# A delta-rule decoder layer on one core: the decay table is scaled on GpSimd, one product per head with the factors repeated along rows, instead of four ScalarE scalings

## The chip, the core and the metric

The kernel runs on one core of one Trainium2 chip. A core has five engines that each work through their own instructions in the order given to them: TensorE (PE in the profile, its weight loads PEld), VectorE (DVE), ScalarE (ACT), GpSimd (POOL) and SyncE (SP), which here only issues transfers. They meet through semaphores. The metric is the device time of one execution in microseconds (us), the median of several runs.

## The reference, cut to what matters

Four sequences of 512 tokens with 512 channels go through a gated delta-rule layer, a cross attention and a layer with self attention and eight experts. Only the first part matters here. For each of 16 heads it runs a recurrence over the tokens:

```python
def step(Sstate, inputs):
    q_t, k_t, v_t, g_t, beta_t = inputs
    retrieved = jnp.einsum('bhkv,bhk->bhv', Sstate, k_t)
    error = v_t - g_t[..., None] * retrieved
    update = k_t[..., :, None] * (beta_t[..., None] * error)[..., None, :]
    Snew = g_t[..., None, None] * Sstate + update
    o_t = jnp.einsum('bhkv,bhk->bhv', Snew, q_t)
    return (Snew, o_t)
```

`q`, `k` and `v` come from projections, a causal convolution over four tokens and SiLU; `q` and `k` are then normed to length one per head. `g` is a decay between 0 and 1, `beta` a gate.

## The kernel before, in words

**Chunks.** The recurrence is computed in chunks of 128 tokens, four to a sequence (`TB` = 4). Within a chunk the errors solve a triangular system. Its matrix is the Gram matrix of the keys, times a table of products of decays, times a factor of the row (`beta` over the squared length of the key). The matrix is inverted, and the state is carried from chunk to chunk by small matmuls.

**Pairs.** Heads are taken two at a time (`HG` = 2), so a sequence has 8 pairs and the batch 32, numbered m = 0 to 31. A pair goes through stages that are spread over several turns of the main loop:

- `stage1(m)` makes keys and queries: `conv` (L533 matmul, L541 first tap on ScalarE, L544 three taps on VectorE, L547 SiLU), the transposed keys and their squared lengths (L576 to L581), the small factor tables `rk`, `ee`, `ke`, `nr` on GpSimd (L588 to L592), the decay tables `em` (L597, a scan on VectorE, one per head), their scaling by `ee` (L602, which calls `scale`), the key products (L606), and the triangular matrix `at` (L609 on VectorE), which is stored (L610) and read back in blocks as `iA` (L673).
- `stage2_inverse(m)` inverts the 32 x 32 diagonal blocks in 31 steps of two small products each (L684, L685), then a turned copy (L691) and transfers (L690 to L698). For even m it runs on VectorE, for odd m on GpSimd (`eng` at L680).
- `stage2_values(m)` makes values and the output gate, with `conv` again (L729, L731, and L537 for the gate).
- `stage3(m)` joins the blocks of the inverse (L765 to L799) and carries the state through the four chunks: L817 (keys times state, into `ps`), L819 (`r` on VectorE), L826 (inverse times `r`), L828 (`u`, copied by ScalarE), L836 (new state's update), L839 (ScalarE, first chunk) or L841 (VectorE, `state` later), and the output matmuls L844 and L846.
- `output(m)` projects a pair (L890) and adds it to the sequence's sum (L893 or L895).

In turn m of the main loop, `stage3(m)` sets the pace, and `turns` advances beside it `output(m - 1)`, two steps of `stage1(m + 2)`, one of `stage2_values(m + 1)`, two of `inversions(m)`, and sometimes the next sequence's `prologue`. `inversions(m)` makes one and two steps of the inverse of pair m + 1 by turns, so three for each turn. So while an even-numbered pair is in `stage1`, GpSimd is inverting an odd-numbered one, and VectorE inverts while an odd-numbered pair is in `stage1`.

**Order.** On VectorE, ScalarE and GpSimd the instructions stand in the order in which the program writes them (`manual_schedule`, L977). The order on TensorE and on the SP queue is made by a scheduler when the kernel is built. `em` has two buffers, one per head; `pb`, the PSUM pool of most matmuls, has four.

`scale` makes four activations, one for each chunk of 128 columns, since ScalarE takes one factor per partition: column p * 4 + c of `ee` for chunk c of head p. `along` views a table of n columns as n blocks, each column repeated:

```python
def along(ap, n):
    return ap.unsqueeze(2).to_broadcast([P, ap.shape[1], n])
```

The same `scale` also makes `kdec` from the transposed keys (`decayed`, L626).

Of the kernel before, what the change touches and what calls it, by code (L numbers as in the profile page):

```python
# [33 lines left out]
ALU = mybir.AluOpType  # L34
# [4 lines left out]
P = 128  # L39
B, S, D = 4, 512, 512  # L40
NT = B * S // P
TB = S // P
# [56 lines left out]
def decoder(ctx: ExitStack, tc: tile.TileContext, a: dict, out: bass.AP):  # L99
    nc = tc.nc  # L100
# [13 lines left out]
    def along(ap, n):  # L114

        return ap.unsqueeze(2).to_broadcast([P, ap.shape[1], n])
# [214 lines left out]
    with ExitStack() as st:  # L331
# [55 lines left out]
        def squares(d):  # L387

            return d[:, : P * P].rearrange("c (r t) -> r c t", r=P)
# [9 lines left out]
        def scale(dst, src, by, p):  # L399

            for c in range(TB):
                nc.scalar.activation(dst[:, c, :], src[:, c, :], AF.Identity, scale=by[:, p * TB + c : p * TB + c + 1])
# [149 lines left out]
        def stage1(m):  # L552
# [31 lines left out]
            rk, ee, ke = (small.tile([P, HG * TB], F32, name=n, bufs=2) for n in ("rk", "ee", "ke"))  # L584
# [8 lines left out]
            em = []  # L593
# [5 lines left out]
                yield  # L599
            ats = []  # L600
            for p in range(HG):
                scale(em[p], em[p], ee, p)  # L602
                pk = p_b.tile([P, TB, P], F32, name="pb")
                for c in range(TB):
                    k_ = kT[p][:, c * P : (c + 1) * P]
                    nc.tensor.matmul(pk[:, c, :], k_, k_, start=True, stop=True)  # L606
                at = live.tile([P, TB, P], F32, name="at", bufs=4)
                ats.append(at)
                nc.vector.scalar_tensor_tensor(at, pk, -1.0, em[p], ALU.mult, ALU.mult)  # L609
                nc.sync.dma_start(squares(at_d[m % SLOTS][p * TB : (p + 1) * TB]), at)  # L610
                yield
# [373 lines left out]

        run(itertools.islice(start, TB + 1))
        pair0 = stage1(0)
        run(turns((start, 1), (itertools.islice(pair0, 2 * HG * 2), 1)))

        run(itertools.islice(pair0, 3 * HG + 1))  # L990
        run(turns((stage2_inverse(0), 2), (chain(pair0, turns((stage1(1), 2), (stage2_values(0), 1))), 1), (prepare(), 1)))
        begun[1] = stage2_inverse(1)
        for m in range(NP):
# [17 lines left out]
            if m + 2 < NP:  # L1011
                if (m + 2) % NHG == 0:
                    assert (m + 2) // NHG in seqs
                rest.append((stage1(m + 2), 2))
# [593 lines left out]
```

## Time and profile before

| what | value |
|---|---|
| median of 3 runs | 3767.66 us (3766.09 to 3770.12) |
| the profiled execution | 3772.63 us, of it 3770.3 us span |
| mean granted TensorE clock | 0.961 |
| ScalarE, L402 on `em` | 256 instructions, 384 to 402 ns, 50.5 to 1939.0 us |
| ScalarE, L402 on `kdec` | 256 instructions, 384 to 408 ns |
| VectorE, L597 scan of `em` | 64 of 1197 to 1444 ns |
| VectorE, L609 `at` | 64 of 668 to 693 ns |
| GpSimd, L588 `rk` | 32 of 1636 to 2492 ns |

The span runs from the first instruction to the last; the profiled execution's own time is 2.3 us more. Times in a timeline are in us from the start of the span. The delta-rule stage fills the first 2000 us or so; the rest is cross attention, self attention and experts. The duration of one instruction holds its start-up and its end, so that neighbours on one engine overlap in the records: eight L402 of 386 ns in a row take 2.45 us together, 306 ns from start to start.

### The profile page before, as it was taken

The page shows a single profiled execution, that of the slowest core. Times are in us where ns is not written, and L with a number is a line of the kernel's source. Part 1 is how long each engine was busy: PE and PEld are TensorE (multiplying, and loading weights), DVE is VectorE, ACT ScalarE, POOL GpSimd, SP SyncE. Part 2 cuts the span into 40 slices and gives each one's busy share as a digit, 9 for nine tenths or more (in the row PEclk, how much of TensorE's full clock was granted, in tenths as well). Part 3 has the DMA queues.
Part 4 walks back from the last instruction along what each step waited for, and adds up shares of the span by engine and source line. Part 5 has one row for each costly group of instructions (what it writes and reads, how often), then busy time and mean ns, then how long its engine had stood idle before and what let it go on. Part 6 is the DMA issues. An engine that isn't in the chain of part 4 may idle for free. (4 is left out here: it accounts for less than half of the span.)

```text
span 3770.3 us, 48773 instructions
## 1 busy us (share of the span) xinstructions
PE 3444.4 (91%) x16466; PEld 1927.3 (51%) x16466; DVE 2205.5 (58%) x4923; ACT 1583.7 (42%) x4379; POOL 1380.1 (37%) x1941
## 2 busy tenths in 40 slices
PE   5889999999899999999997799998999999898897
PEld 3545555555555555555554455555555555554443
DVE  5667667776677666765674466555655655554111
ACT  3444444444444444444442244444444444343121
POOL 1444554356444553455543222112112111211442
PEclk8999999999999999999998799999999999999998
DMA  5333332534244342333341445445444544446444
GB/s 157 108 100 117 103 113 85 147 101 122 85 118 126 100 122 91 116 119 118 96 127 37 157 155 162 136 148 145 141 137 137 160 147 136 147 151 209 87 84 92
DMA packets 391879, 465.54 MB, mean 123 GB/s; under 512 B 128451, under 2 KB 242115, under 8 KB 391440
## 3 DMA queue, kind: packets, MB, share of 16 engines
q1 hardware_dynamic: 380080, 438.03, 38.0%
q0 software_dynamic: 10112, 21.58, 3.1%
q8 instruction: 131, 2.15, 0.2%
q10 hardware_dynamic: 1440, 2.84, 0.2%
q14 instruction: 116, 0.95, 0.1%
HBM read 401.76 MB, written 64.81 MB: 124 GB/s over the span
## 5 line engine op out<-in xcount | busy, mean ns | idle before, releaser
L533 PE MATMUL pb<-xnT,w 128*128 128x512 f32 x2048 | 973.5, 610 | 20.3 <-issue 9.9
L533 PEld LDWEIGHTS pb<-xnT,w 128*128 128x128 f32 x2048 | 374.6, 195 | 420.2 <-issue 401.1
L544 DVE SCALAR_TENSOR_TENSOR cv<-pb,pp,cv 128x510 f32<-128x510 f32 (+2 forms) x576 | 423.3, 744 | 29.2 <-ACT cv L541 16.9
L1145 PE MATMUL pb<-c_q,hT 128*128 128x512 f32 x768 | 361.3, 609 | 6.7 <-DMA c_q<-in_c_wk_dram 3.1
L685 POOL TENSOR_TENSOR iT<-iT,iW 32x31 f32<-32x31 f32 (+15 forms) x496 | 275.8, 556 | 38.9
L684 POOL TENSOR_TENSOR iW<-iA,iT 32x31 f32<-32x31 f32 (+15 forms) x496 | 250.0, 504 | 58.8 <-DMA iA<-at_d 15.6
L890 PE MATMUL pb<-wot,og 128*128 128x512 f32 x512 | 251.0, 613 | 2.0 <-issue 1.5
L1251 PE MATMUL pw<-c_o,oT 128*128 128x512 f32 x512 | 240.9, 601 | 1.0 <-DVE oT L1243 1.0
L1145 PEld LDWEIGHTS pb<-c_q,hT 128*128 128x128 f32 x768 | 143.5, 195 | 162.3 <-issue 151.5
L1217 ACT ACTIVATE e<-pb,nm,rq 128x128 f32<-128x128 f32 (+3 forms) x256 | 157.0, 619 | 141.3 <-DVE nm L1215 112.9
L541 ACT ACTIVATE cv<-pb,pp 128x512 f32<-128x512 f32 x192 | 148.6, 774 | 158.4 <-PE pb L533 155.5
L685 DVE TENSOR_TENSOR iT<-iT,iW 32x31 f32<-32x31 f32 (+15 forms) x496 | 203.7, 411 | 17.0
L640 POOL TENSOR_TENSOR qg<-qh,row 128x512 f32<-128x512 f32 x64 | 82.7, 1292 | 357.7 <-ACT qh L547 313.3
L684 DVE TENSOR_TENSOR iW<-iA,iT 32x31 f32<-32x31 f32 (+15 forms) x496 | 185.5, 374 | 42.7 <-DMA iA<-at_d 32.1
L279 POOL TENSOR_SCALAR x_e<-x_e 128x1024 f32<-128x1024 f32 x64 | 67.2, 1050 | 340.6 <-ACT x_e L274 259.6
L588 POOL TENSOR_TENSOR rk<-ss,mhalf 128x8 f32<-128x8 f32 x32 | 66.7, 2085 | 340.5 <-DVE ss L587 339.6
L895 DVE TENSOR_TENSOR xa<-pb,xa 128x512 f32<-128x512 f32 x112 | 76.9, 687 | 195.4 <-PE pb L890 195.4
L1241 PE MATMUL po<-eT,val 128*128 128x512 f32 x320 | 169.6, 623 | 11.0 <-ACT eT L1239 8.4
L274 ACT ACTIVATE x_e<-pb,nm 128x256 f32<-128x256 f32 x256 | 118.3, 476 | 128.2 <-DVE nm L271 122.2
L1211 PE MATMUL pb<-kT,qT 128*128 128x256 f32 (+3 forms) x576 | 162.6, 409 | 0.0
L1513 PE MATMUL pb<-w_gu,eT 128*128 x312 | 142.9, 602 | 3.5 <-issue 3.5
L547 ACT ACTIVATE qh<-cv 128x512 f32<-128x512 f32 x64 | 40.3, 630 | 249.7 <-DVE cv L544 237.3
(330 smaller groups left out, 6503.4 us busy)
## 6 DMA issues: line engine op xcount, KB each, us to landing
c_o<-in_c_wo_dram SPq DMA_DIRECT2D x128, 512.0 KB, 4.1
c_q<-in_c_wq_dram SPq DMA_DIRECT2D x128, 512.0 KB, 4.7
w<-in_a_w_dram SPq DMA_DIRECT2D x124, 512.0 KB, 3.6
row<-g_d SPq DMA_DIRECT2D x64, 512.0 KB, 3.6
at_d<-at SPq DMA_DIRECT2D x64, 256.0 KB, 2.7
T<-t_d SPq DMA_DIRECT2D x32, 512.0 KB, 4.3
X<-x_d SPq DMA_DIRECT2D x32, 512.0 KB, 5.2
rrow<-r_d SPq DMA_DIRECT2D x32, 512.0 KB, 3.7
```

The costliest lines, as they stand in the source:

```text
L533: nc.tensor.matmul(pj, wt[:, kd, p * P : (p + 1) * P], xnT[:, kd, :], start=kd == 0, stop=kd == KD - 1)
L541: nc.scalar.activation(ac, pj, AF.Identity, bias=cb[:, m, h : h + 1], scale=cw[:, m, h, 3:4])
L544: nc.vector.scalar_tensor_tensor(ac[:, j:], pj[:, : S - j], cw[:, m, h, 3 - j : 4 - j], ac[:, j:], ALU.mult, ALU.add)
L684: eng.tensor_tensor(u, A[:, i, i + 1 :].unsqueeze(2).to_broadcast([nb, n, w]), T[:, i, :w].unsqueeze(1).to_broadcast([nb, n, w]), ALU.mult)
L685: eng.tensor_tensor(T[:, i + 1 :, :w], T[:, i + 1 :, :w], u, ALU.add)
L890: nc.tensor.matmul(pw, og[p][:, c * P : (c + 1) * P], wot[:, p, :], start=p == 0, stop=p == HG - 1)
L1145: nc.tensor.matmul(pj, hT[:, kd, :], w[:, kd % 2, :], start=kd == 0, stop=kd == KD - 1)
L1211: nc.tensor.matmul(ps[:, m, k * P : (k + w) * P], qT[g][:, n + m, :], kT[:, g, j : j + w, :], start=True, stop=True)
L1217: nc.scalar.activation(e[n + m][:, :nk], ps[:, m, :nk], AF.Exp, bias=nm[:, n + m : n + m + 1], scale=rq, accum_out=es[:, n + m : n + m + 1])
L1241: nc.tensor.matmul(po, val[:, g, :], eT, start=k == 0, stop=k == c)
L1251: nc.tensor.matmul(pw, oT[:, h + m, :], w[:, m, :], start=g == 0 and h + m == 0, stop=g == 3 and h + m == 3)
L1513: nc.tensor.matmul(pg, hT[:, kd, :], w_gu[:, bass.ds(e, 1), kd, :, :], start=kd == 0, stop=kd == KD - 1)
```

## The change

One line of `stage1` changes. For each head p, the table `em[p]` (128 partitions by 4 chunks of 128 columns) was multiplied in place by four ScalarE activations; now one GpSimd product of two tensors does it, with the four factors of the head read through a view that repeats each along 128 columns.

```diff
@@ -599,7 +599,7 @@
                 yield
             ats = []
             for p in range(HG):
-                scale(em[p], em[p], ee, p)
+                nc.gpsimd.tensor_tensor(em[p], em[p], along(ee[:, p * TB : (p + 1) * TB], P), ALU.mult)
                 pk = p_b.tile([P, TB, P], F32, name="pb")
                 for c in range(TB):
                     k_ = kT[p][:, c * P : (c + 1) * P]
```

`kdec` is still scaled on ScalarE.

## The prediction

> **What bounds the kernel now.** I read the page's shares first, then the wait lists of the stretch in which `em` is made (0 to 1990 us), then the timelines around one pair.
>
> ```profile
> PE 3444.4 (91%) x16466; PEld 1927.3 (51%) x16466; DVE 2205.5 (58%) x4923; ACT 1583.7 (42%) x4379; POOL 1380.1 (37%) x1941
> 1260.00:1320.00 60.00, 55.43 (x292) 31.71 (x292) 44.22 (x87) 26.76 (x77) 27.57 (x38) 0.97 0.37 111
> ```
>
> The second line is a 60 us window of the delta-rule stage: TensorE is busy for 55.4 us of it, ScalarE for 26.8, GpSimd for 27.6. TensorE is the bound, and its order is fixed. So time is gained or lost only where TensorE waits, and a free ScalarE is worth what it takes out of those waits. The lists, with total us, number and longest:
>
> ```profile
> PE pb L576 <- ACT kT L547: 40.8, 31, 2.7
> PE ps L836 <- ACT u L828: 25.2, 12, 2.7
> ...
> DVE at L609 <- ACT em L402: 73.3, 42, 4.9
> ...
> ACT em L402 <- POOL ee L590: 135.2, 31, 6.2
> ```
>
> The scaling stands in the middle of two queues. ScalarE sits 135 us before it until GpSimd has `ee`, VectorE sits 73 us at `at` until ScalarE is done. TensorE's part is the second line: `u` (L828) stands behind the scaling on ScalarE. The 32 pairs fall into two kinds by what GpSimd does before `ee`. In odd pairs it is free and `ee` comes 0.9 us after the scans. In even pairs from 4 on it is inverting, and `ee` comes 3.0 to 4.1 us after the scans. Pair 20, one of these, one timeline for each engine:
>
> ```profile
> 1274.23 2.45 ACT L402 ACTIVATE em<-em,ee 128x128 f32<-128x128 f32 x8 [5.46 <-POOL ee L590]
> 1276.59 0.76 ACT L541 ACTIVATE cv<-pb,pp 128x512 f32<-128x512 f32 x1
> 1277.25 0.41 ACT L828 COPY u<-ps 128x128 f32<-128x128 f32 x2
> ```
>
> ```profile
> 1273.99 0.20 POOL L590 TENSOR_TENSOR ee<-ee,beta 128x8 f32<-128x8 f32 x1
> ...
> 1274.43 0.20 POOL L592 TENSOR_TENSOR nr<-ss,rk 128x8 f32<-128x8 f32 x1
> 1274.72 0.36 POOL L684 TENSOR_TENSOR iW<-iA,iT 32x112 f32<-32x112 f32 x1
> ...
> 1276.83 0.29 POOL L685 TENSOR_TENSOR iT<-iT,iW 32x60 f32<-32x60 f32 x1
> ```
>
> ```profile
> 1275.54 0.69 DVE L609 SCALAR_TENSOR_TENSOR at<-pb,em 128x512 f32<-128x512 f32 x1 [3.86 <-ACT em L402]
> 1276.71 0.69 DVE L609 SCALAR_TENSOR_TENSOR at<-pb,em 128x512 f32<-128x512 f32 x1 [0.48 <-ACT em L402]
> 1277.46 1.53 DVE L544 SCALAR_TENSOR_TENSOR cv<-pb,pp,cv 128x511 f32<-128x511 f32 x2
> 1278.91 0.60 DVE L841 SCALAR_TENSOR_TENSOR state<-state,gall,ps 128x128 f32<-128x128 f32 x2
> ```
>
> ```profile
> 1272.06 3.60 PE L533 MATMUL pb<-xnT,w 128*128 128x512 f32 x8
> 1277.55 0.96 PE L836 MATMUL ps<-u,kdec 128*128 128x128 f32 x4 [1.89 <-ACT u L828]
> ...
> 1280.00 1.06 PE L817 MATMUL ps<-state,kT 128*128 128x128 f32 x4
> 1280.85 3.81 PE L533 MATMUL pb<-xnT,w 128*128 128x512 f32 x8
> ```
>
> Read them together: L836 waits 1.89 us for `u`; L817 needs `state` of L841, and L841 stands on VectorE behind both `at` and two taps of L544. From here all times are from the end of `ee` (1274.19 in this pair).
>
> **What goes.** 256 ScalarE instructions, 98.8 us by their mean of 386 ns, in groups of eight that take 2.45 us, and the idle time ahead of them. In pair 20 `u` could then follow L826 (1271.59) at once, and L836 starts when the eight L533 are through, near +1.4 instead of +3.36. That takes the wait at L836 away: 1.88 to 2.70 us in each of 11 even pairs, 24.6 us in all.
>
> **What comes.** 64 GpSimd products of 128x512. The trace has this kind of operation, a product with a factor repeated along the row, in L222: median 1.05 us. The bounds are 1.05 below and 1.28 above (L640, two full operands, same size); I take 1.05, the row with the same view. For two heads that is 2.18 us with the 0.08 us between GpSimd's instructions, so no longer than ScalarE's 2.45. The Trainium skill (GPSIMD Engine Reference, 4.1 Engine selection) speaks against such a move: products of two inputs belong on VectorE, since GpSimd takes about twice its time. By that rule GpSimd is the wrong place; by the rows a head costs 1.05 us on GpSimd and 1.22 in four pieces on ScalarE, which is what it replaces. I go by the rows and put nothing on the duration.
>
> **Where it is put is what costs.** GpSimd's order in the changed kernel is `nr`, then in odd pairs `em` twice. In even pairs three steps of the inverse stand between, because `stage1` gives way after its two scans and a turn has three steps. In pair 20 these are the instructions from 1274.72 to 1277.12. So `em[0]` runs from +3.0 to +4.05 and `em[1]` to +5.2, where ScalarE was done at +2.5. On VectorE the second `at` starts at +5.25 instead of +2.52, **2.7 us later**, and everything behind it waits: taps (1.46 us), then `state`. The second `at` ends at 5.9, taps end at 7.4, the first `state` at 7.7, so L817 starts at **+7.8 instead of +5.8**. TensorE idles from about +2.8 to +7.8, 5 us in place of 1.9. The wait is not removed, it changes engine and grows.
>
> By kind of pair:
> - Pairs 4, 12, 20, 28, 30, as above: 2.0 us each, 10 us.
> - Pairs 6, 8, 14, 16, 22, 24 have steps of the next sequence's norms or gates ahead of `state` on VectorE; L817 already starts as soon as `state` is there (+6.42 in pair 22), so it moves by the whole 2.7: 16 us.
> - Pairs 10, 18, 26 (output norms beside): there L533 waits 3.3 us, and in pair 18 it starts at 1156.60, just when the first `at` (1155.81 + 0.69) has read its PSUM buffer. That `at` is 2.75 us later: 8 us.
> - Pair 2: the three steps are the longest ones and last from 172.83 to 177.13. The second `at` ends at 180.1, L817 goes from 178.35 to 182.0: 3.7 us.
> - Odd pairs: `em[1]` is ready at about +2.7. Half of them read it later anyway (`at` starts at +2.19 or after, without a wait); the others lose 0.2 us: 1 us.
>
> **The clock.** After the wait in pair 20 the small matmuls of L844 take 0.64 us for two, and 0.39 elsewhere: TensorE restarts at half speed. From L836 to L729 five such pairs lose 0.5 to 1.4 us; the pairs 10, 18, 26, which idle 3.3 us, need 6.09, 6.26 and 5.24 us for eight L533 instead of 3.60, a loss of 2.3 us. The Trainium skill (TensorE: Matmul & The Clock Gate, Part 1) says that the clock halves after an idle window of about 3.4 us, free-running, and returns after a busy one. By the rule alone the old waits of 1.9 us could have cost nothing and the new 5 us would add up to 1.7 each (an estimate, half of that window); the rows show that waits of 1.9 us do cost. I go by the rows: 2.3 us after the longer idle time, less the 0.6 to 0.8 us that are lost after L817 already, so 1.5 us for each of the 11 pairs, 17 us, and 2.3 in pair 2.
>
> **What gives back.** Five even pairs wait again at L621 for `qh` (0.3 to 2.4 us), behind the load of `iA`, which moves with `at` by some 2.8 us and so by less than TensorE does: 3 us. Otherwise no slack is left: the later waits, L576 in every pair, are a chain TensorE to ScalarE to VectorE to ScalarE that starts from TensorE's own matmul.
>
> **Other edges.** On GpSimd, what stands behind `em` (the last step, L691, L849, L640) is 2.2 us later; the next `stage3` reads the inverse some 20 us after L691, and `qg` two turns later. On SP the order changes too: both stores of `at` now stand together, and a weight load that stood between them goes behind the load of X. It is 10 us later (1276.74 becomes about 1287), for weights that the next turn reads, whose `stage3` begins near 1303. I price both at nothing; if that cover failed, L533 would wait for its weights.
>
> **Sum.** 10 + 16 + 8 + 4 + 1 = 39; clock 19; back 3: **+55 us**. On the profiled execution, 3772.6, that is 3828; on the median of the runs, 3767.7, it is **3823 us**.
>
> **Rivals.**
> 1. *Faster, because ScalarE's queue is free* (chance 0.05). If VectorE did not hold L817, the waits at L836 (24.6 us) and the half-speed matmuls after them (about 1.2 us in 11 pairs) go: 3767.7 - 38 = 3730 us. It decides at one point: L817 follows `em[1]` by 2.6 us, so `em[1]` would have to be ready before +3.2. For: ScalarE's 135 us. Against: three steps of the inverse, 2.5 us, stand ahead of the products.
> 2. *No change* (0.05): the late `at` falls beside TensorE's other work, 3768 us. Against: L817 stands ahead of the L533 in TensorE's order, and that order is the same after the change.
> 3. *GpSimd is held up by VectorE* (0.10). Beside the scans a step of L685 took 1.36 us in place of 0.49, and one L849 took 2.31. If each product took 2.3, the second `at` would be another 2.5 us later in 15 pairs: 3860 us. Against: VectorE stands idle at `at` in just these pairs.
>
> My forecast has 0.80. Without any more clock loss it gives 3803; with 1.28 us for a product (+7), 2.66 us of clock loss (+4) and nothing given back (+3) it gives 3837. The range 3796 to 3846 takes in both and a little of rival 3. A difference under 0.2% (7.5 us) can't be told from none here: slower 0.91, same 0.04, faster 0.05.
>
> **What would show it.** In even pairs the wait of L836 for `u` is gone and L817 waits some 5 us for `state`; VectorE's wait at `at` names POOL and grows by 2.7 us; the `em` products take about 1.05 us; the granted clock of the stage falls a little. I am wrong if L817 starts before +6, or if the products stand directly behind `nr` in time.

## The result, and the profile after

The changed kernel takes **3827.2 us** (median of 4 runs, 3823.5 to 3834.0), the kernel before, on the same chip, 3768.9 (4 runs, 3766.1 to 3774.0): ratio 1.0155, 95% interval 1.0137 to 1.0173. It is slower by 58 us. The profiled execution took 3823.5 us with a span of 3820.9 (before 3770.3) and a mean granted TensorE clock of 0.953 (before 0.961).

The first row of the page (busy time, share, instructions) and the list of TensorE's waits in the first 2025 us (total us, number, longest), changed kernel:

```profile
PE 3456.0 (90%) x16466; PEld 1932.2 (51%) x16466; DVE 2215.3 (58%) x4923; ACT 1511.7 (40%) x4123; POOL 1440.4 (38%) x2005
```

```profile
PE ps L817 <- DVE state L841: 47.3, 15, 5.2
...
PE pb L442 <- DVE x_in L137: 27.8, 4, 9.8
PE pb L533 <- issue: 18.0, 3, 6.0
...
PE pb L481 <- DVE lg L475: 12.3, 3, 4.6
```

ScalarE did 72 us less and GpSimd 60 us more, as intended. The wait of L836 for `u` (25.2 us before) has left the list, and in its place L817 waits 47.3 us for `state`. L533's three waits grew from 9.9 to 18.0 us. Two lines were not in the forecast: L442 (the next sequence's transposes) waits 27.8 us for VectorE's L137, of which the first 9.8 stand at the kernel's start and were there before under another name, so 18.0 us in three waits are new; and L481 (the next sequence's gates) waits 12.3 instead of 7.5.

Pair 20 after the change, one timeline for each engine; `ee` ends at 1303.14 here:

```profile
1304.47 0.61 PE L836 MATMUL ps<-u,kdec 128*128 128x128 f32 x4
...
1310.65 1.22 PE L817 MATMUL ps<-state,kT 128*128 128x128 f32 x4 [4.67 <-DVE state L841]
1311.65 4.82 PE L533 MATMUL pb<-xnT,w 128*128 128x512 f32 x8
```

```profile
1303.66 0.36 POOL L684 TENSOR_TENSOR iW<-iA,iT 32x112 f32<-32x112 f32 x1
...
1306.13 2.04 POOL L602 TENSOR_TENSOR em<-em,ee 128x512 f32<-128x512 f32 x2
```

```profile
1307.21 0.69 DVE L609 SCALAR_TENSOR_TENSOR at<-pb,em 128x512 f32<-128x512 f32 x1 [6.57 <-POOL em L602]
1308.20 0.69 DVE L609 SCALAR_TENSOR_TENSOR at<-pb,em 128x512 f32<-128x512 f32 x1 [0.30 <-POOL em L602]
```

Read from top to bottom: L836 follows at +1.33 without a wait (+3.36 before), but GpSimd reaches the products only at +2.99, behind three steps of the inverse; the second `at` starts at +5.06 (+2.52 before) and L817 at +7.51 (+5.81 before). That is the mechanism of the forecast in its own numbers.

Where the 50.6 us of span went is best seen from pair to pair. For each pair I took the time from the end of its `ee` (L590) to the end of the next one's, in both traces:

| pairs | change, us | forecast (waits and clock) |
|---|---|---|
| 4, 12, 20, 28, 30 | +9.7 | 17.5 less 3 given back |
| 8, 16, 24 | +7.5 | 12.6 |
| 6, 14, 22 | +18.1 | 12.6 |
| 10, 18, 26 | +11.6 | 8 |
| 2 | -1.0 | 6 |
| odd, but for 1, 7, 15, 23 | -0.6 | 1 for all odd pairs |
| 1, 7, 15, 23 | +8.7 | |
| ahead of pair 1, and behind the last `ee` | -3.3 | 0 |

The sum is right, but the rows are off by up to 8 us either way. Two of those that lost more called for a cause that the forecast does not have: **pairs 6, 14, 22, and pairs 1, 7, 15, 23, which were to cost next to nothing and lost 8.7 us**. The experiments had to test the main mechanism and find these.

### The profile page after: what moved, and what is told of

Its sections match the earlier page's. It is cut to its first block, busy times and chain, and to the rows that moved or that the text cites. A ratio compares the mean times of both kernels' runs of the same rounds, so it can differ in the third digit from the quotient of the medians.

```text
span 3820.9 us, 48560 instructions
## 1 busy us (share of the span) xinstructions
PE 3456.0 (90%) x16466; PEld 1932.2 (51%) x16466; DVE 2215.3 (58%) x4923; ACT 1511.7 (40%) x4123; POOL 1440.4 (38%) x2005
## 5 line engine op out<-in xcount | busy, mean ns | idle before, releaser
L533 PE MATMUL pb<-xnT,w 128*128 128x512 f32 x2048 | 990.7, 619 | 28.5 <-issue 18.0
L533 PEld LDWEIGHTS pb<-xnT,w 128*128 128x128 f32 x2048 | 380.8, 199 | 437.6 <-issue 416.5
L544 DVE SCALAR_TENSOR_TENSOR cv<-pb,pp,cv 128x510 f32<-128x510 f32 (+2 forms) x576 | 423.4, 744 | 28.5 <-ACT cv L541 17.2
L685 POOL TENSOR_TENSOR iT<-iT,iW 32x31 f32<-32x31 f32 (+15 forms) x496 | 274.3, 553 | 38.9
L685 DVE TENSOR_TENSOR iT<-iT,iW 32x31 f32<-32x31 f32 (+15 forms) x496 | 202.5, 408 | 17.1
```

The lines of the kernel that those rows point to most:

```text
L533: nc.tensor.matmul(pj, wt[:, kd, p * P : (p + 1) * P], xnT[:, kd, :], start=kd == 0, stop=kd == KD - 1)
L544: nc.vector.scalar_tensor_tensor(ac[:, j:], pj[:, : S - j], cw[:, m, h, 3 - j : 4 - j], ac[:, j:], ALU.mult, ALU.add)
L685: eng.tensor_tensor(T[:, i + 1 :, :w], T[:, i + 1 :, :w], u, ALU.add)
```

## The experiments

Theory A: an even pair loses by the time at which its second `em` is ready, and that is late because the products stand behind three steps of the inverse in GpSimd's order. Rivals: the product costs wherever it stands; or the loss comes from VectorE, the memory ports or the clock. All ratios are to the kernel before, on the same chip.

### Products ahead of the steps of the inverse

```diff
                 em.append(e)
-                yield
+            for p in range(HG):
+                nc.gpsimd.tensor_tensor(em[p], em[p], along(ee[:, p * TB : (p + 1) * TB], P), ALU.mult)
+            yield
+            yield
             ats = []
             for p in range(HG):
-                scale(em[p], em[p], ee, p)
```

> Both GpSimd products stand directly behind `nr`, ahead of the two turns' breaks, so no step of the inverse stands between; the operation and its engine are those of the change. My theory (the place in GpSimd's queue costs, through VectorE's queue): in even pairs em[1] is ready near +2.5 us from the end of `ee`, the second `at` starts there as it did before the change, L817 comes at about +5 instead of +7.5, and the time falls to 3755 to 3772 us. Rival A (a product on GpSimd costs by itself, by its operand view or by sharing ports with VectorE): the time stays near 3827. Rival B (the new orders on TensorE and SP cost): it stays above 3800.

Measured: 3789.2 us, ratio 1.0038 (1.0024 to 1.0052). Most of the loss is gone, and the time is below what either rival allowed (about 3827, or above 3800). The plain even pairs (4, 12, 20, 28, 30) are back at 57.0 to 58.2 us from `ee` to `ee` (57.1 to 58.9 before the change, 59.5 to 60.3 after it). But it is 14 us slower than before, outside what A expected: in the profiled execution, which was the slowest of the five, pairs 1, 7, 15 and 23 still had 11.4 us of it, and pairs 14 and 22 another 8.0. A explains the larger part, and something else is in the odd pairs.

### The place alone, without GpSimd's products

ScalarE scales as before; `rk`, `ee`, `ke` and `nr` move behind the two steps of `stage1`, and so behind the three steps of the inverse.

```diff
-            nc.gpsimd.tensor_tensor(rk, ss, mhalf[:, 0 : HG * TB], ALU.pow)
...
-            nc.gpsimd.tensor_tensor(nr, ss, rk, ALU.mult)
             em = []
...
                 yield
+            nc.gpsimd.tensor_tensor(rk, ss, mhalf[:, 0 : HG * TB], ALU.pow)
...
+            nc.gpsimd.tensor_tensor(nr, ss, rk, ALU.mult)
             ats = []
```

> The scaling stays on ScalarE as before the change, but the five small GpSimd tables (rk, ee, ee, ke, nr) stand behind the two breaks, so in even pairs three steps of the inverse stand ahead of them. My theory: ScalarE is done 2.5 us later than before the change, the second `at` starts near where it does in the changed kernel, L817 comes 1.5 to 2.5 us later than before the change, and the time is 3810 to 3840 us, without any GpSimd product of `em`. Rival A (the product on GpSimd costs by itself): about 3769, as before the change.

Measured: 3813.1 us, ratio 1.0103 (1.0086 to 1.0120). Not one product stands on GpSimd, and 38 us are lost. The timeline of TensorE for pair 20 of this kernel shows the same gap in the form that belongs to ScalarE:

```profile
1303.38 1.23 PE L836 MATMUL ps<-u,kdec 128*128 128x128 f32 x4 [4.37 <-ACT u L828]
```

The wait for `u` is 4.37 us where it was 1.89. So the place alone costs most of it, whichever engine scales.

### Odd pairs alone, even pairs alone

```diff
-                scale(em[p], em[p], ee, p)
+                if m % 2:
+                    nc.gpsimd.tensor_tensor(em[p], em[p], along(ee[:, p * TB : (p + 1) * TB], P), ALU.mult)
+                else:
+                    scale(em[p], em[p], ee, p)
```

> Only odd pairs scale on GpSimd, even ones on ScalarE. My theory: odd pairs have no step of the inverse in between and cost at most 0.3 us each, so 3765 to 3775 us. Rival A (each GpSimd product costs): half of the 58 us, about 3798.

> Only even pairs scale on GpSimd, odd ones on ScalarE. My theory: nearly the whole cost, 3815 to 3832 us. Rival A: half of it, about 3798.

(The second has `m % 2 == 0`.) Measured: odd pairs alone 3790.1 us, ratio 1.0035 (1.0022 to 1.0047), a miss: odd pairs cost 13 to 15 us, not nothing. Even pairs alone 3822.2 us, ratio 1.0129 (1.0112 to 1.0146), as expected. So even pairs alone cost 47 us and odd pairs alone 15: two causes.

### A slope: `em` later still

In even pairs two more GpSimd instructions for each head stand ahead of its product.

```diff
+                for _ in range(2 if m % 2 == 0 else 0):
+                    nc.gpsimd.tensor_scalar(em[p], em[p], 1.0, 0.0, ALU.mult, ALU.add)
                 nc.gpsimd.tensor_tensor(em[p], em[p], along(ee[:, p * TB : (p + 1) * TB], P), ALU.mult)
```

> The changed kernel, and in even pairs two more GpSimd instructions for each head (the table times 1.0 plus 0.0) just ahead of its product, so that the second em is ready four instructions later: by half of L279's 1.05 us (128x1024) about 2.1 us. A slope: if the time at which em is ready sets the pace of even pairs, each of 16 loses about 2.1 us more, 14 to 16 of them in full: 3827 + 29 to 34, with up to 10 more where TensorE's clock falls: 3850 to 3870. Rival (the loss comes from the memory ports or the clock and not from the time at which em is ready): under 3840.

Measured: 3871.0 us, ratio 1.0267 (1.0251 to 1.0283), 1 us above the expected range. The timeline of GpSimd for pair 20 has two added instructions in 1.31 us where I had estimated 1.05:

```profile
1338.93 1.31 POOL L603 TENSOR_SCALAR em<-em 128x512 f32<-128x512 f32 x2
...
1342.73 1.04 POOL L604 TENSOR_TENSOR em<-em,ee 128x512 f32<-128x512 f32 x1
```

So the second `em` is 2.8 us later than in the changed kernel (1343.77 - 1338.93 = 4.84 for what took 2.04), and 16 x 2.8 = 45 us: measured 3871.0 - 3827.2 = 44 (42 by the two ratios). In the sum the even pairs pay one for one for the time at which `em` is ready. By pair it is less even: most lost 1.9 to 3.5 us more, pairs 2, 14 and 22 4.6 to 4.7, and pairs 10 and 18, where L533 waits for the first `at`, whose `em` is only 1.4 us later, 1.2; pair 26 lost nothing.

### The odd pairs: which of them

First all odd pairs but those beside which the next sequence's gates are made (and pair 1), then only those.

```diff
-                scale(em[p], em[p], ee, p)
+                if m % 2 and m % NHG != NHG - 1 and m != 1:
+                    nc.gpsimd.tensor_tensor(em[p], em[p], along(ee[:, p * TB : (p + 1) * TB], P), ALU.mult)
+                else:
+                    scale(em[p], em[p], ee, p)
```

> Only odd pairs on GpSimd, as in the run of odd pairs alone, but without pairs 1, 7, 15, 23 (and 31), beside which the next sequence's gates are made. Theory (the 13 us of odd pairs come from VectorE's small steps of the gates, slowed beside a GpSimd product of two inputs): 3765 to 3777 us, as before. Rival (the products cost about 0.8 us in every odd pair): 11 of 16 are left, so 3778 to 3787.

> Only pairs 1, 7, 15, 23 and 31 on GpSimd, as in the changed kernel; all others on ScalarE. Together with the run of the other odd pairs this is the run of all odd pairs. Theory (VectorE's small steps of the next sequence's gates take several times as long beside a GpSimd product of two inputs, so TensorE waits longer at L481): 3 to 4 us in each of four pairs: 3782 to 3791 us. Rival (place in the sequence does not matter): 5 of 16 of the 13 us: 3777 to 3779.

(The second has `m % NHG == NHG - 1 or m == 1`.) Measured: eleven odd pairs 3774.1 us, ratio 1.0003 (0.9994 to 1.0012), so those products are free. The other five, 3783.9 us, ratio 1.0036 (1.0023 to 1.0050): the whole cost of the odd pairs, in five of 16. Pair 23 of this kernel, timelines of GpSimd, VectorE and TensorE (the edit moves lines behind 602 down by three, so L688 here is L685 of before):

```profile
1467.10 2.04 POOL L603 TENSOR_TENSOR em<-em,ee 128x512 f32<-128x512 f32 x2
1469.09 1.26 POOL L852 TENSOR_TENSOR gs<-gs,rrow 128x512 f32<-128x512 f32 x1
```

```profile
1467.09 1.11 DVE L688 TENSOR_TENSOR iT<-iT,iW 32x60 f32<-32x60 f32 x1
1468.13 1.07 DVE L470 SCALAR_TENSOR_TENSOR sp_y<-sp_y,sp_z 128x64 f32<-128x64 f32 x1
1469.24 1.16 DVE L471 TENSOR_SCALAR sp_y<-sp_y 128x64 f32<-128x64 f32 x1
1470.43 0.23 DVE L472 SCALAR_TENSOR_TENSOR sp_y<-g_a,sp_y 128x64 f32<-128x64 f32 x1
```

```profile
1471.20 1.55 PE L481 MATMUL pb<-lg,tab_a 128*128 128x64 f32 x6 [3.30 <-DVE lg L475]
...
1473.50 4.86 PE L533 MATMUL pb<-xnT,w 128*128 128x512 f32 x7
```

Three small VectorE instructions take 1.1 us each, where their like need 0.20 to 0.23. Add start and duration: they end at 1468.20, 1469.20 and 1470.40; the first product ends at about 1468.14 (1467.10 + 1.04), the second at 1469.14, L852 at 1470.35. **Each VectorE instruction ends just behind one GpSimd instruction: it does not run slowly, it is held until that one is over**, and the next is caught by the next. In the kernel before, only L849 (L852 above) stood there and caught one, L470. The same place in pair 23 before, GpSimd and VectorE:

```profile
1459.60 1.34 POOL L849 TENSOR_TENSOR gs<-gs,rrow 128x512 f32<-128x512 f32 x1
```

```profile
1459.59 0.21 DVE L685 TENSOR_TENSOR iT<-iT,iW 32x60 f32<-32x60 f32 x1
1459.73 1.29 DVE L470 SCALAR_TENSOR_TENSOR sp_y<-sp_y,sp_z 128x64 f32<-128x64 f32 x1
1461.06 0.20 DVE L471 TENSOR_SCALAR sp_y<-sp_y 128x64 f32<-128x64 f32 x1
```

So `lg` comes 1.6 us later after `ee` (+4.45 for +2.81), L481 starts late, and the eight L533 that follow run at a lower granted clock (0.68 for 0.84; they take 5.28 us for 4.27). The Trainium skill has the rule (SBUF — State Buffer, Who interferes with whom): the two engines share one pair of ports as an exclusive lock; whichever starts first keeps it for its whole instruction, and VectorE needs it for two SBUF inputs or in its fast modes. The held instructions agree with it; which of two started first the records cannot show (L688's start is written 0.01 us ahead of the product's), nor whether L471, which reads one tensor, ran in such a mode.

Pair 1 is another matter. There is no gate work; GpSimd's L222, which waits for VectorE's L221, stands ahead of the products, and in the same run the first `at` starts at +2.76 after `ee` instead of +1.35. That is theory A again, in an odd pair. Pair 15 hides its loss: in the table it is 0.4 us shorter, because it took 66.5 us in the trace of before, while the other runs that leave it as it was have 63.3 to 64.8; after the change it took 66.1.

### The same products in short pieces

Held until the instruction ends, or slowed in proportion? The same five pairs, each product as four of 128 columns:

```diff
-                scale(em[p], em[p], ee, p)
+                if m % NHG == NHG - 1 or m == 1:
+                    for c in range(TB):
+                        nc.gpsimd.tensor_tensor(em[p][:, c : c + 1, :], em[p][:, c : c + 1, :], along(ee[:, p * TB + c : p * TB + c + 1], P), ALU.mult)
+                else:
+                    scale(em[p], em[p], ee, p)
```

> Pairs 1, 7, 15, 23 and 31 on GpSimd, as in the run of these pairs alone, but each product as four of 128 columns. Theory (a VectorE instruction with two SBUF inputs, or a fast one, is held until the one GpSimd instruction that is under way has ended, as L471 and L472 ended 0.05 to 0.1 us after a product or an L849): a piece lasts about 0.4 us (an estimate: (1.04 - 0.20) / 4 + 0.20), so L470 to L475 take 0.3 to 0.5 us each, L475 ends at about +3.0 after ee (+4.5 with whole products, +2.8 before): 3768 to 3779 us. Rival (VectorE is slowed in proportion while GpSimd works on the same memory, however its work is cut): pieces are GpSimd's busy time made longer (3.3 us for 2.1), so as before or worse: 3782 to 3795.

Measured: 3770.9 us, ratio 1.0003 (0.9995 to 1.0012). Pair 23, GpSimd and VectorE:

```profile
1452.64 2.90 POOL L604 TENSOR_TENSOR em<-em,ee 128x128 f32<-128x128 f32 x8
```

```profile
1453.04 0.43 DVE L470 SCALAR_TENSOR_TENSOR sp_y<-sp_y,sp_z 128x64 f32<-128x64 f32 x1
1453.51 0.30 DVE L471 TENSOR_SCALAR sp_y<-sp_y 128x64 f32<-128x64 f32 x1
1453.84 0.35 DVE L472 SCALAR_TENSOR_TENSOR sp_y<-g_a,sp_y 128x64 f32<-128x64 f32 x1
...
1454.59 0.29 DVE L475 TENSOR_SCALAR lg<-sp_y 128x64 f32<-128x64 f32 x1
```

GpSimd is busy for 2.90 us instead of 2.04, yet VectorE's steps take 0.3 to 0.4 us, `lg` is ready at +2.63 after `ee`, and the 13 us are gone. More GpSimd work in shorter instructions costs less. Slowing in proportion is ruled out. Pair 1 still loses 3.5 us here, as it should if its cause is the queue.

### Other places and engines

Even pairs: both products on GpSimd directly behind `ee`, ahead of `ke` and `nr`; odd pairs on ScalarE:

```diff
+            for p in range(0 if m % 2 == 0 else HG, HG):
+                nc.gpsimd.tensor_tensor(em[p], em[p], along(ee[:, p * TB : (p + 1) * TB], P), ALU.mult)
+            nc.gpsimd.tensor_tensor(ke, ee, flat(gend), ALU.mult)
+            nc.gpsimd.tensor_tensor(nr, ss, rk, ALU.mult)
+            yield
+            yield
             ats = []
             for p in range(HG):
-                scale(em[p], em[p], ee, p)
+                if m % 2:
+                    scale(em[p], em[p], ee, p)
```

> Even pairs: both GpSimd products directly behind the end of ee, ahead of ke, nr and the steps of the inverse. Odd pairs: ScalarE as before. Theory (the changed kernel loses by the three steps of the inverse ahead of the products in even pairs, and by products beside the next sequence's gates in odd pairs): neither is left. em[1] ready at +2.1 after ee, second at from +2.15, L817 at about +4.7 (5.1 to 5.8 before), the wait of L836 for u gone: 3755 to 3773 us. Rival (each GpSimd product costs something wherever it stands, since GpSimd's own chain or the memory ports get fuller): 3785 or more.

Measured: 3777.7 us, ratio 1.0013 (1.0004 to 1.0022). Both causes are undone and the loss with them, but nothing is won: the plain even pairs are at 57.0 to 58.0 us, about as before. The time is 5 us above what was expected. In its profile pairs 14 and 22 take 4.0 and 2.0 us more than before, and pairs 10, 18, 26 1.2 to 1.4 each; no run here shows why.

A variant of it in which VectorE scales head 0 of even pairs, by one product at the old place, and GpSimd only head 1:

```diff
-            for p in range(0 if m % 2 == 0 else HG, HG):
+            for p in range(1 if m % 2 == 0 else HG, HG):
...
                 if m % 2:
                     scale(em[p], em[p], ee, p)
+                elif p == 0:
+                    nc.vector.tensor_tensor(em[p], em[p], along(ee[:, p * TB : (p + 1) * TB], P), ALU.mult)
```

> Even pairs: head 0 scaled by one VectorE product at the old place, head 1 by one GpSimd product directly behind the end of ee. Odd pairs: ScalarE as before. Theory (VectorE's second at is what everything waits for, and VectorE is idle there): both at are done by about +2.8, L817 at about +4.0, so 1 to 1.8 us gained in some 11 even pairs: 3748 to 3768 us, and below the kernel before. Rival (TensorE's next wait, for L576 or L533, takes it back): 3765 to 3775. Rival (the two engines' products in the same span slow each other): over 3780.

Measured: 3769.4 us, ratio 0.9994 (0.9984 to 1.0005), no difference: the hoped-for gain did not come. In pair 22, L442 waits 0.90 and L817's counterpart 1.98 us, where L836 had waited 2.70; L621's waits rose from 10.2 to 13.9 us. The wait moved on along TensorE's order, as the first rival said, though to these three places and not to L576 or L533, which it named.

All pairs on VectorE:

```diff
-                scale(em[p], em[p], ee, p)
+                nc.vector.tensor_tensor(em[p], em[p], along(ee[:, p * TB : (p + 1) * TB], P), ALU.mult)
```

> All pairs: the product of a head on VectorE, at the old place just ahead of its at; ScalarE and GpSimd do none of it. Theory (only the time at which the second at ends counts, whichever engine makes em): in even pairs 2 x 1.05 + 2 x 0.69 = 3.5 us of VectorE after ee, where the second at ended at +3.2 before, so L817 at +5.6 to +6.0, about as before, and the wait of L836 gone: 3760 to 3785 us. Rival (any move off ScalarE costs, since VectorE is the fuller engine): VectorE gains 64 x 1.05 = 67 us of work and a third or more of it shows: 3790 to 3835.

Measured: 3773.7 us, ratio 0.9996 (0.9987 to 1.0005). VectorE does 43 us more work (2248.5 for 2205.5) and nothing shows: most even pairs are 0.4 to 2.6 us shorter, the plain odd ones 0.6 to 1.4 longer, and so are pairs 14 and 22, by 2.7. So I kept the good half, without the pairs beside the next sequence's norms:

```diff
+                if m % 2 == 0 and m % NHG != NHG - 2:
+                    nc.vector.tensor_tensor(em[p], em[p], along(ee[:, p * TB : (p + 1) * TB], P), ALU.mult)
+                else:
+                    scale(em[p], em[p], ee, p)
```

> Even pairs, except those beside the next sequence's norms (6, 14, 22, 30): each head scaled by one VectorE product at the old place. All other pairs: ScalarE as before. Theory (in the run with all pairs on VectorE the even pairs gained about 1 us each and the odd ones lost 0.7 us each, which cancelled): 12 pairs x 1.0: 3757 to 3766 us, ratio 0.996 to 0.9985. Rival (odd pairs take back what even pairs gain, since the next wait moves too): 3769 to 3775, no difference from before.

Measured: **3759.6 us, ratio 0.9975 (0.9966 to 0.9984)**, 11 us faster than before and the only version here that beats it. VectorE in pair 20, where `ee` ends at 1258.61:

```profile
1258.64 0.69 DVE L603 TENSOR_TENSOR em<-em,ee 128x512 f32<-128x512 f32 x1 [2.54 <-POOL ee L590]
1259.37 0.69 DVE L612 SCALAR_TENSOR_TENSOR at<-pb,em 128x512 f32<-128x512 f32 x1
1259.98 0.68 DVE L603 TENSOR_TENSOR em<-em,ee 128x512 f32<-128x512 f32 x1
1260.77 0.69 DVE L612 SCALAR_TENSOR_TENSOR at<-pb,em 128x512 f32<-128x512 f32 x1
```

The product takes 0.69 us here against 1.04 on GpSimd and 1.22 in four ScalarE pieces, on an engine that stood idle at just this place. The second `at` starts at +2.16 (+2.52 before), and L817 at +4.61 (+5.81).

## Why the prediction held, and where its sizes were off

The direction, the mechanism and the sum were right: 3823 us forecast, 3827 measured. By its steps:

- **What goes.** L836's waits (24.6 us forecast) are gone; L836 starts at +1.33 in pair 20, forecast +1.4.
- **The product's duration.** 1.04 us, forecast 1.05 from L222; two heads take 2.04, forecast 2.18. The same product takes 0.69 us on VectorE, so GpSimd needs 1.5 times as long here and not about twice, as in the rule that the prediction cites.
- **The place.** Products from +2.99 (forecast +3.0), `em[1]` ready at +5.03 (+5.2), second `at` at +5.06 (+5.25), L817 at +7.51 (+7.8), TensorE idle for 4.67 us (5). The run with the tables moved and the slope show that this time sets the pace.
- **Plain even pairs.** L817 moved by 1.7 us in pairs 4 and 20 and by 2.4 in 12, 28 and 30: 10.6 in all, forecast 10. Given back at L621 were 5.2 us (10.2 to 5.0), not 3.
- **Pairs 8, 16, 24.** The reading was wrong: no norms or gates of the next sequence stand ahead of `state` there. VectorE's order in all three is `at`, `at`, L544, L841, as in pair 20. L817 moved by 2.4, 2.4 and 1.4 us, forecast 2.7 each.
- **The clock.** TensorE's busy time for the same 9500 matmuls or so, up to 1975 us before and 2025 us after, rose by only 8.7 us (1797.6 to 1806.3), forecast 19. But this is a sum of two. From L836 to L846 it fell by 6 us in the even pairs, as the old wait is gone; that saves nothing, since L817 comes later anyhow. From L817 to the next `ee`, which the forecast priced, it rose by 16 us. So the sum was nearly right and the places were not. The plain even pairs have 1.0 us each, forecast 1.5. Pairs 8, 16, 24 have 1.3 in all, forecast 4.5: in pair 8 the eight L533 had already been slow before (4.64 us, now 4.98). Pairs 14 and 22 have 4 us each (granted clock 0.92, before 0.97 and 0.99), and pairs 10, 18, 26, priced at nothing, have 3.3 in all.
- **Pairs 10, 18, 26.** The waits at L533 grew by 8.1 us, forecast 8; with the clock they lost 11.6 in all. Pair 26 has 5.5 of that, against 4.0 with even pairs alone, so part of it varies from run to run.
- **Pair 2.** Forecast 6 us, measured -1.0: L817 does come 3.4 us later and waits 3.2, but L765 later waits 4.1 us less for a transfer. I had not looked so far along the pair.
- **Odd pairs.** Forecast 1 us in all. Plain ones gained 0.3 us or lost 0.4; pairs 1, 7, 15, 23 lost 8.7. Of that, 3.1 are pair 1's, by the queue (L222 ahead of the products). In the other three my third rival had asked whether VectorE holds up GpSimd, and I looked only in that direction: beside the products it was **GpSimd that held up VectorE**.
- **The weight load on SP, the later end of the inverse.** Priced at nothing; no wait of TensorE's names either. But L691, part of that later end, is what L137 meets in pairs 6, 14, 22 (below).

**Pairs 6, 14, 22: the step that was mis-sized.** "L817 already starts as soon as `state` is there (+6.42 in pair 22), so it moves by the whole 2.7". It moved by 4.2 in pair 22 (+6.42 to +10.65): by 2.5 for the later `at`, and by 1.7 because VectorE's L137, which stands between `at` and `state`, took that much longer. TensorE waits 5.99 us for L137 at L442 and then 1.52 for `state` at L817. VectorE's L137 in pair 22 before, then two timelines of the changed kernel, VectorE and GpSimd:

```profile
1396.47 0.54 DVE L137 TENSOR_SCALAR x_in<-x_in,ln_mv,ln_rs 128x512 f32<-128x512 f32 x1
```

```profile
1429.48 2.23 DVE L137 TENSOR_SCALAR x_in<-x_in,ln_mv,ln_rs 128x512 f32<-128x512 f32 x1
```

```profile
1429.53 1.89 POOL L691 COPY iA<-iT 32x1024 f32<-32x1024 f32 x1
```

Moved 2.5 us later, L137 now stands beside GpSimd's L691 and ends 0.29 us behind it, in all three pairs with 2.23 us. I take it for the same holding as in the odd pairs; here it is read from the trace and was not tried by itself. Two runs agree: with even pairs alone on GpSimd, L442 has the same three waits (18.0 us); with the products ahead of the steps, L137 stands beside short steps again and takes 0.58 us, and L442 waits 1.8 us each time. In pairs 14 and 22 the lower clock comes on top.

So the mechanism was right, but that 3823 came so close to 3827 is luck. The errors nearly cancelled: too much for pair 2, for pairs 8, 16, 24 and for the plain even pairs, too little for VectorE's instructions caught behind GpSimd's and for the clock in pairs 10, 14, 18, 22 and 26.

## What to carry to other kernels

When an operation moves to another engine, find its new neighbours in that engine's order before comparing durations: a product that was no slower cost 1.3% here in the even pairs (47 us), for the most part because three short steps stood ahead of it. Then list what the other engines run beside it at the new time, and what runs beside whatever is pushed back. A long GpSimd instruction can hold a VectorE instruction of 0.2 us for its whole length; shorter GpSimd instructions, even with more time in all, can remove that cost.

## What the runs showed of the hardware that I had not expected

- A VectorE instruction of 0.20 to 0.23 us with two SBUF inputs took 1.06 to 1.22 us beside a GpSimd product of 1.04 or 1.26 us and ended some 0.05 to 0.1 us behind it, up to three in a row. So did `TENSOR_SCALAR`, which reads one tensor: L471 with 0.94 to 1.16 us, and L137 with 2.23 us, 0.29 us behind a copy of 1.89. The record shows VectorE as busy, not as waiting.
- L609, which reads one input from PSUM, kept its 0.67 to 0.69 us beside GpSimd's products.
- Cut into eight pieces of 128 columns, the two products take 2.90 us instead of 2.04.
